# Layer 2's node norms regrouped: late tiles normalised in SBUF with their product and sum on POOL, second norms shared by ACT and DVE

## The chip, the cores and the metric

The kernel runs on one core of one Trainium2 chip. A core has TensorE (PE) for matrix products, VectorE (DVE), ScalarE (ACT) and GpSimd (POOL) for elementwise work, and DMA queues; SP issues plain transfers here and POOL issues the gathers. Each engine works through its own instructions in the order in which they stand, and waits for others by semaphores. SBUF is the on-chip memory of 128 partitions, PSUM the memory into which TensorE writes. The metric is the device time of one execution in microseconds, as the median of several runs; lower is better.

## The reference

Four graph layers work on `x` (8 batches, 2048 nodes, 64 features) with one adjacency matrix. Each layer's output is added to `x`, and the sum is normalised over the features. Only layer 2, the third, is touched:

```python
A = (adj_matrix > 0).astype(x.dtype)
agg = jnp.einsum('ij,bjf->bif', A, x) / jnp.maximum(deg, 1.0)[None, :, None]
out = jax.nn.relu(x @ W_self + b_self + (agg @ W_neigh + b_neigh))
mu = out.mean(axis=-1, keepdims=True)
var = jnp.mean((out - mu) ** 2, axis=-1, keepdims=True)
out = (out - mu) * jax.lax.rsqrt(var + LN_EPS) * ln_gamma + ln_beta   # the first norm
x = _layernorm(x + out, axis=-1)                                      # the second norm
```

## The kernel before

The 2048 nodes are 16 tiles of 128. `X[:, t]` and `S[:, t]` hold tile t in SBUF as 8 batches of 64 features. Before the part in question, each tile of `X` has been turned and multiplied with the weights; `S` holds the self term and `ytab` in memory the neighbours' rows, and `b2` (the norm's beta) has already been added to `X` (line 761).

The neighbour sums of tiles 0 to 8 are made with the adjacency as a matrix (PE, line 899, 144 steps of three matmuls), those of tiles 15 down to 9 with edge lists: `fetch` has POOL issue four gathers of rows of `ytab` for each third of such a tile (helper line 186), and `add_edges` multiplies them with a selection matrix (PE, line 879). The two kinds run interleaved in one loop over the 144 steps.

When a tile's sum in `pa` is complete, `finish` (lines 842 to 854) scales it by the degree and adds the self term (line 844), applies relu (845) and takes statistics with four `bn_stats` (line 780). Tiles that are finished one after the other are put together in groups, whose sizes are in the list `sizes`; a full group starts a `chain`. The order of finishing is 0, 15, 1, 14, 2, 3, 13, 4, 12, 5, 11, 6, 10, 7, 9, 8, and with the sizes 1, 2, 3, 4, 3, 1, 1, 1 the groups are (0), (15, 1), (14, 2, 3), (13, 4, 12, 5), (11, 6, 10), (7), (9), (8).

A `chain` (lines 795 to 823) is a Python generator that emits its instructions piece by piece:

- `newton` (lines 768 to 776): 1/sqrt(variance) for the whole group on DVE, twelve small dependent steps (lines 773, 123, 126 to 128, 775);
- the first norm of each tile, one instruction per batch, from `S` to a PSUM tile `z` (two of these exist, pool `pz`): `scaled` has ACT do it (line 788), or, in a chain that starts when fewer than two sizes are left, DVE every second batch (line 786, argument `shared`): in the trace these are the chains of tiles 7, 9 and 8;
- the product with `g2` (line 809) and the sum with `X` (line 810) on DVE, then statistics of `X` and `newton` again;
- the second norm, in place in `X`, again through `scaled`;
- `show` (lines 825 to 832): POOL copies the tile into one of three buffers `Xo` (line 828) and SP writes it to the table `xtab` in three DMAs (lines 829 and 832).

`advance` moves the chains on: three pieces are emitted for every two steps of the loop, the rest after it, and between pieces come the other matmuls, finishes and gathers. Everything is in a manually scheduled block, so each engine's order is that in which the instructions are emitted: a finish that is emitted after a chain's piece waits behind it on DVE, and gathers emitted after a `show` wait behind its copy on POOL. Beside the steps, PE, ACT and DVE also prepare layer 3: `own_scores` with its DVE reduction (line 701) and `set_shifts` (PE line 705, DVE lines 706 and 710).

After the loop, layer 3 begins with two products (`sides`, PE line 954) whose PSUM results ACT and DVE copy into `U` (lines 963 and 964), and with gathers from `xtab` (the helper's line 186 again, tile `xs`). The gathers need all rows of `xtab`. Instructions of `sides` come into the engines' orders where the planner puts them, not always behind all of layer 2.

Of the kernel before, what the change touches and what calls it, by code (L numbers as in the profile page):

```python
# [21 lines left out]
F32 = mybir.dt.float32  # L22
# [5 lines left out]
AF = mybir.ActivationFunctionType  # L28
ALU = mybir.AluOpType
# [3 lines left out]
P = 128  # L33
# [15 lines left out]
def kernel(ctx: ExitStack, tc: tile.TileContext, ins: dict, out: bass.AP):  # L49
    nc = tc.nc  # L50
    x, adj = ins["x"], ins["adj"]
    B, N, D = x.shape
# [27 lines left out]
    def rows(name, src, pool):  # L80

        n = src.shape[0]
        t = pool.tile([P, n], F32, name=name)
        nc.sync.dma_start(t, src.unsqueeze(0).to_broadcast([P, n]))
        return t

    def over(v, shape):

        for _ in shape[1:-1]:
            v = v.unsqueeze(1)  # L90
        return v.to_broadcast(shape)
# [70 lines left out]
    X = main.tile([P, NT, B, D], F32, name="X")  # L162
# [97 lines left out]
    def node_products(t0, wk, ps):  # L260
# [26 lines left out]
        for q, ph in enumerate(held):  # L287
# [26 lines left out]
                                   op0=ALU.is_equal, op1=ALU.mult)  # L314
# [8 lines left out]
    for it in range(NT):  # L323
# [18 lines left out]
        for k in range(0, SL, 8):  # L342
            nc.vector.max(nbr[:, k:k + 8], topf)
            if k + 8 < SL:
# [19 lines left out]
                                       op0=ALU.is_le, op1=ALU.mult, saturate=False)  # L364
# [27 lines left out]
    held, zs, stats = {}, {}, {}  # L392
# [108 lines left out]
    with ExitStack() as l1:  # L501
# [60 lines left out]
        def finish(it, po):  # L562
            for h in range(2):
                rec = wk.tile([P, HB * D], F32, name="rec")
                nc.vector.reciprocal(rec, po[h][:, 0])  # L565
                nc.vector.tensor_tensor(po[h][:, 1], po[h][:, 1], rec, ALU.mult)
                Xs = X[:, it, h * HB:(h + 1) * HB, :].rearrange("p b d -> p (b d)")
                nc.vector.tensor_tensor(Xs, po[h][:, 1], Xs, ALU.add)
            done.add(it)
            if it ^ 1 in done:  # L570
                layer_norm([X[:, t] for t in (it & ~1, it | 1)], wk)
# [12 lines left out]
        for it in range(FIRST):  # L584
            finish(it, sums[it])
# [13 lines left out]
        def add_edges(n):  # L599
            it, s = quads[n]  # L600
            if s == 0:
                selfs[it] = wk.tile([P, GS, P], F32, name="self_")
                nc.scalar.activation(selfs[it], Sel[:, it], AF.Copy)
                sums[it] = new_sums()
            for h in range(2):
                for g in range(NG):
                    nodes = slice(g * GN, (g + 1) * GN)
                    nc.tensor.matmul(sums[it][h][nodes].rearrange("p a f -> p (a f)"), selfs[it][:, s, nodes],  # L608
                                     rss[n][g][:, h], start=(s == 0), stop=(s == GS - 1))
            if s == GS - 1:  # L610
                finish(it, sums[it])
# [6 lines left out]
        for k, (it, jt) in enumerate(steps):  # L618
            if jt == 0:
                sums[it] = new_sums()  # L620
            add_rows(sums[it], it, jt)
            if jt == NT - 1:
                finish(it, sums[it])
            while n < len(quads) and n * (len(steps) - LATE - EARLY) <= (k - LATE) * len(quads):
                add_edges(n)
                fetch(n + 2)
                n += 1
# [84 lines left out]
    with ExitStack() as l2:  # L712
# [12 lines left out]
        g2 = rows("g2", ins["L2_gnn_ln_gamma"], wp)  # L725
# [7 lines left out]
        S = wp.tile([P, NT, B, D], F32, name="S")  # L733
# [31 lines left out]
        pz = l2.enter_context(tc.tile_pool(name="l2pz", bufs=2, space=PSUM))  # L765
        sums, rss, selfs, shown = {}, {}, {}, []

        def newton(st):

            n = st.shape[1]  # L770
            triples = st.rearrange("p n a (k m) -> p (n a k) m", m=3)
            var, rstd, tmp, nmr = (small.tile([P, 4 * B], F32, name=f"l2_{k}", bufs=4)[:, 0:n * B] for k in "vrtm")
            nc.vector.scalar_tensor_tensor(var, triples[:, :, 2], 1.0 / D, eps.to_broadcast(var.shape), op0=ALU.mult, op1=ALU.add)
            inv_sqrt(rstd, var, tmp)
            nc.vector.scalar_tensor_tensor(nmr, triples[:, :, 1], -1.0, rstd, op0=ALU.mult, op1=ALU.mult)
            return rstd, nmr

        def take_stats(st, k, v):
            for a in range(NP):
                nc.vector.bn_stats(st[:, k, a], v[:, 2 * a:2 * a + 2, :].rearrange("p b d -> p d b"))  # L780

        def scaled(to, v, stats, k, b, shared):
            rstd, nmr = stats
            own = slice(k * B + b, k * B + b + 1)
            if shared and b % 2:
                nc.vector.tensor_scalar(to[:, b], v[:, b], rstd[:, own], nmr[:, own], op0=ALU.mult, op1=ALU.add)
            else:
                nc.scalar.activation(to[:, b], v[:, b], AF.Identity, scale=rstd[:, own], bias=nmr[:, own])  # L788


        sizes = [1, 2, 3, 4, 3, 1, 1, 1]
        together, chains = [], []
        WAIT = 3

        def chain(ts, st):


            shared = len(sizes) < 2
            stats = newton(st)
            for _ in range(WAIT):  # L800
                yield False
            st = small.tile([P, 4, NP, 6], F32, name="l2_sx")[:, 0:len(ts)]
            for k, t in enumerate(ts):
                z = pz.tile([P, B, D], F32, name="z")
                for b in range(B):
                    scaled(z, S[:, t], stats, k, b, shared)
                    if b % 2:
                        yield True
                nc.vector.tensor_tensor(z, z, over(g2, [P, B, D]), ALU.mult)
                nc.vector.tensor_tensor(X[:, t], z, X[:, t], ALU.add)  # L810
                take_stats(st, k, X[:, t])
            stats = newton(st)
            for _ in range(WAIT):
                yield False
            for k, t in enumerate(ts):
                for b in range(B):
                    scaled(X[:, t], X[:, t], stats, k, b, shared)
                    if b % 2:
                        yield True
                    if b == 1 and k:  # L820
                        show(ts[k - 1])
            yield False
            show(ts[-1])

        def show(t):
            Xo = ones_x[len(shown) % len(ones_x)]
            shown.append(t)
            nc.gpsimd.tensor_copy(Xo[:, :, 1:], X[:, t, :, 1:])
            nc.sync.dma_start(xtab[t * P:(t + 1) * P, 0:BD // 2], Xo[:, 0:B // 2].rearrange("p b d -> p (b d)"))
            pair_of = xtab[t * P:(t + 1) * P, BD // 2:].rearrange("n (a k d) -> n a k d", k=2, d=D)  # L830
            for k_ in range(2):
                nc.sync.dma_start(pair_of[:, :, 1 - k_], Xo[:, B // 2 + k_::2])
# [9 lines left out]
        def finish(it):  # L842
            sf = S[:, it].rearrange("p b d -> p (b d)")
            nc.vector.scalar_tensor_tensor(sf, sums.pop(it), r_deg[:, it:it + 1], sf, op0=ALU.mult, op1=ALU.add)
            nc.vector.tensor_scalar(sf, sf, 0.0, None, op0=ALU.max)
            if not together:
                together.append((small.tile([P, 4, NP, 6], F32, name="l2_st")[:, 0:sizes[0]], []))
            st, ts = together[0]
            take_stats(st, len(ts), S[:, it])
            ts.append(it)  # L850
            if len(ts) == sizes[0]:
                sizes.pop(0)
                together.pop()
                chains.append(chain(ts, st))

        by_list = list(range(NT - 1, DENSE - 1, -1))
        quads = [(it, s) for it in by_list for s in range(GS)]
# [78 lines left out]
    with early, ExitStack() as heads:  # L936
# [190 lines left out]
        with tc.manual_schedule(engines=engines):  # L1127
# [22 lines left out]
            t = NT - 1  # L1150
# [10 lines left out]
    with ExitStack() as fifth:  # L1161
# [17 lines left out]
        hss, pes, ws, wxs, zs, stats, sums = ({} for _ in range(7))  # L1179
# [116 lines left out]
        with tc.manual_schedule(engines=engines):  # L1296
# [5 lines left out]
            for u in range(len(units) + 7):  # L1302
# [19 lines left out]
                for plan, t0, t1 in ((after, 0, PAIRED - 2), (sooner, PAIRED - 2, PAIRED)):  # L1322
                    for j, fs in plan.items():
                        k = u - j - 2 * PER + 1
# [3 lines left out]
                for j, fs in alone.items():  # L1328
                    k = u - j - PER + 1
# [35 lines left out]
    with tc.If(bad > 0), ExitStack() as anyway:  # L1365
# [12 lines left out]
        X = main.tile([P, NT, B, D], F32, name="X")  # L1378
# [13 lines left out]
        with tc.tile_pool(name="adjp", bufs=3) as ap_, tc.tile_pool(name="adjps", bufs=4, space=PSUM) as aps:  # L1392
            for it in range(NT):
# [15 lines left out]
                own = ap_.tile([P, P], F32, name="own")  # L1409
# [44 lines left out]
        with ExitStack() as l0:  # L1454
# [71 lines left out]
            for b in range(B):  # L1526
                p, k = divmod(b, 2)
# [8 lines left out]
                for ih in range(2):  # L1536
                    acc = [pa.tile([P, CW], F32, name="acc") for _ in range(2)]
                    for jt in range(NT):
                        w = pp.tile([P, HW], F32, name="w")
                        nc.vector.tensor_scalar(w, F[:, ih * HW:(ih + 1) * HW], Cj[:, jt, b:b + 1], Aj[:, jt, b:b + 1],  # L1540
                                                op0=ALU.mult, op1=ALU.max)
                        nc.vector.scalar_tensor_tensor(w, MT[:, jt, ih * HW:(ih + 1) * HW], 0.0, w,
                                                       op0=ALU.is_equal, op1=ALU.mult)
# [11 lines left out]
                if k == 1:  # L1555
                    for c in range(NCH):
# [4 lines left out]
                        ts = slice(c * TPC, (c + 1) * TPC)  # L1561
                        Xs = X[:, ts, 2 * p:2 * p + 2, :].rearrange("p t b d -> p t (b d)")
                        v = wk.tile([P, TPC, P], F32, name="v", tag="t2")
# [92 lines left out]
        with ExitStack() as l2:  # L1656
# [12 lines left out]
            g2 = rows("g2", ins["L2_gnn_ln_gamma"], wp)  # L1669
            b2 = rows("b2", ins["L2_gnn_ln_beta"], wp)  # L1670

            S = wp.tile([P, NT, B, D], F32, name="S")
# [34 lines left out]
        with ExitStack() as l3:  # L1707
# [44 lines left out]
            bias = wp.tile([D, HN + 1], F32, name="bias")  # L1752
# [149 lines left out]
```

## Time and profile before

| What | us |
|---|---|
| median of five runs | 2067.24 |
| lowest and highest run | 2062.77, 2070.85 |
| the profiled execution: time | 2072.89 |
| the profiled execution: its span | 2071.1 |
| first matmul of layer 2's neighbour sums (line 899) | 823.1 |
| last such matmul begins (line 899) | 976.5 |
| last copy into `Xo` begins (line 828) | 1015.14 |
| first gather of layer 3 (tile `xs`) | 1021.13 |

Over the whole span PE is busy 75%, DVE 68%, POOL 51% and ACT 49%. These shares are means over stages with different limits. Costs of the instructions concerned, as mean or median durations of one:

| Instruction | engine | ns |
|---|---|---|
| line 788, scaling a batch, into `z` (PSUM) | ACT | 408 |
| line 788, scaling a batch, in `X` (SBUF) | ACT | 426 |
| line 786, the same, into `z` | DVE | 347 |
| line 786, the same, in `X` | DVE | 308 |
| lines 809 and 810, product and sum of a tile | DVE | 698, 691 |
| lines 1271 and 1276, product and sum of a tile in layer 3 | POOL | 1277, 1264 |
| line 828, copy of a tile | POOL | 607 |
| line 186, issuing a gather | POOL | 957 |

Instructions in a row overlap a little, so the time from one to the next can be shorter than the duration of one: 32 scalings in `X` on ACT take 10.71 us in a row, 0.335 us each.

### The profile page before, as it was taken

The numbers are of one execution on the slowest core, as the hardware profiler recorded it, in microseconds if no ns is written. First come the engines' busy times: TensorE is split into PE (matmuls) and PEld (weight loads), VectorE is DVE, ScalarE is ACT, GpSimd is POOL, SyncE is SP. The second block draws the span as 40 slices with busy tenths as digits, with TensorE's granted clock in tenths as the row PEclk, the third lists the DMA queues.
The fourth block names the chain that finished last, engine by engine and source line by source line (L and its number), as shares of the span: only waits on it lengthen the run. The fifth ranks groups of instructions, "written<-read, shape, count | busy, mean of one in ns | idle before, by whom it ended". The sixth has DMA issues, their size and how long they took to land.

```text
span 2071.1 us, 35059 instructions
## 1 busy us (share of the span) xinstructions
PE 1557.4 (75%) x13026; PEld 897.7 (43%) x13062; DVE 1414.2 (68%) x3057; ACT 1024.4 (49%) x2504; POOL 1065.1 (51%) x993
## 2 busy tenths in 40 slices
PE   3572344442799987997299999999999689888873
PEld 3562121110333335332188787787787522222210
DVE  6879388886665456557555655656565489889886
ACT  4553144356822234347255545445455246777774
POOL 0000777761655526563245656556555287777760
PEclk9975555665999999999599999999999855555555
DMA  7321666660248942564233323323333165655541
GB/s 198 128 95 61 194 200 206 205 181 24 99 164 294 301 144 89 163 193 122 76 99 109 115 86 109 107 91 109 102 99 111 59 186 154 175 165 166 158 120 22
DMA packets 134243, 283.65 MB, mean 137 GB/s; under 512 B 64145, under 2 KB 66705, under 8 KB 131985
## 3 DMA queue, kind: packets, MB, share of 16 engines
q0 software_dynamic: 64896, 217.10, 34.8%
q1 hardware_dynamic: 52528, 60.03, 8.7%
q10 hardware_dynamic: 16640, 4.20, 0.9%
q8 instruction: 105, 1.72, 0.3%
q14 instruction: 74, 0.60, 0.1%
HBM read 245.35 MB, written 35.91 MB: 136 GB/s over the span
## 4 chain that ended last, share of the span: by engine, by line
PE 38%; DVE 11%; ACT 9%; issue 6%; POOL 6%; DMA 2%; SPq 0%; ACTq 0%; POOLq 0%; DVEq 0%
PE pscore L999 7%; PE pa L556 6%; PE po L1025 6%; PE pt L984 5%; POOL hs L186 3%; PE pm L954 3%; PE pm L1060 3%; PE pa L608 2%; PE pa L899 2%; DVE sc L1204 2%; PE po L1232 1%; ACT z L151 1%; DVE pr L1199 1%; ACT wx L1215 1%; ACT z L788 1%
## 5 line engine op out<-in xcount | busy, mean ns | idle before, releaser
L186 POOL DMA_INDIRECT hs<-htab,src x192 | 183.7, 957 | 269.9 <-PE pe L408 207.5
L1008 DVE SCALAR_TENSOR_TENSOR w<-w,Sel 128x512 f32<-128x512 f32 (+1 forms) x192 | 188.8, 1010 | 173.8 <-ACT w L1002 173.3
L186 POOL DMA_INDIRECT xs<-xtab,src x192 | 221.2, 1152 | 66.9 <-issue 29.7
L556 PE MATMUL pa<-R,ET 128*128 128x512 bf16 x841 | 196.3, 387 | 53.9 <-POOL R L544 34.8
L186 POOL DMA_INDIRECT hs<-ktab,src x192 | 188.6, 982 | 53.8 <-issue 45.8
L999 PE MATMUL pscore<-U,xsT 64*128 64x64 f32 (+1 forms) x3072 | 204.6, 280 | 0.0
L1002 ACT ACTIVATE w<-pscore 128x1024 f32<-128x1024 f32 x128 | 130.9, 1023 | 137.3 <-PE pscore L999 130.2
L999 PEld LDWEIGHTS pscore<-U,xsT 64*128 64x128 f32 x3072 | 183.5, 189 | 21.7 <-issue 15.0
L986 ACT COPY xsT<-pt 128x512 f32<-128x512 f32 x192 | 112.1, 584 | 142.2 <-PE pt L984 140.4
L151 ACT ACTIVATE X<-X,ln_m,ln_r 128x64 f32<-128x64 f32 x256 | 87.2, 427 | 171.4 <-DVE ln_m L143 171.4
L1194 PE MATMUL pe<-hi,selTb 32*128 32x512 bf16 x576 | 135.2, 603 | 35.6 <-DVE pr L1199 34.9
L556 PEld LDWEIGHTS <-ET 128*128 128x128 fp8e4 x864 | 84.1, 99 | 174.5 <-issue 82.8
L1025 PE MATMUL po<-w,xs 128*64 128x64 f32 (+1 forms) x3072 | 143.7, 243 | 16.5 <-DVE o L1030 16.5
L1070 POOL TENSOR_TENSOR h<-h,h2h 128x512 f32<-128x512 f32 x45 | 57.2, 1270 | 165.5 <-DVE h2h L1066 165.3
L1025 PEld LDWEIGHTS po<-w,xs 128*64 128x64 f32 x3072 | 119.5, 137 | 43.9 <-DVE o L1030 18.8
L984 PE MATMUL pt<-ident,xs 128*128 128x128 f32 x768 | 127.8, 290 | 7.7 <-DMA xs<-xtab,src 6.3
L1215 ACT ACTIVATE wx<-hs,w 128x64 f32<-128x64 f32 x512 | 128.7, 341 | 0.1
L1199 DVE TENSOR_TENSOR pr<-pe,hs 128x1024 f32<-128x1024 f32 x96 | 116.7, 1216 | 16.8 <-DMA hs<-ktab,src 10.5
L1204 DVE TENSOR_REDUCE sc<-pr 128x16 f32<-128x1024 f32 x96 | 116.5, 1214 | 4.7 <-ACT w L1206 1.2
L186 POOL DMA_INDIRECT rs<-rtab,src x84 | 79.6, 948 | 71.9 <-PE pa L608 51.8
L565 DVE RECIPROCAL rec<-pa 128x256 f32<-128x256 f32 x32 | 54.1, 1728 | 78.0 <-PE pa L608 48.4
L428 DVE TENSOR_TENSOR hs<-hs,w 128x2048 f32<-128x2048 f32 x48 | 106.7, 2277 | 0.5 <-ACT w L418 0.5
(592 smaller groups left out, 3275.1 us busy)
## 6 DMA issues: line engine op xcount, KB each, us to landing
at<-in_adj SPq DMA_DIRECT2D x16, 1024.0 KB
rtab<-r SPq DMA_DIRECT2D x16, 512.0 KB
ptab<-hp SPq DMA_DIRECT2D x16, 384.0 KB
hi<-ptab SPq DMA_DIRECT2D x16, 384.0 KB
X<-in_x ACTq DMA_DIRECT2D x16, 256.0 KB
htab<-H SPq DMA_DIRECT2D x16, 256.0 KB
ytab<-y SPq DMA_DIRECT2D x16, 256.0 KB
ktab<-hb SPq DMA_DIRECT2D x16, 256.0 KB
```

Of the source, the lines that this page charges most:

```text
L186: nc.gpsimd.indirect_dma_start(out=dst, out_offset=None, in_=table[:, :], in_offset=bass.IndirectOffsetOnAxis(ap=src[:, it, s, g:g + 1], a ...
L556: nc.tensor.matmul(po[h].rearrange("p a f -> p (a f)"), ET[:, jt, it * P:(it + 1) * P], R[:, jt, q, h].rearrange("p a f -> p (a f)"), star ...
L984: nc.tensor.transpose(pt[:, p], xss[k][n][:, p * P:(p + 1) * P], ident)
L986: nc.scalar.copy(xsT, pt)
L999: nc.tensor.matmul(pscore[:, k_, f0:f0 + HN * ni].rearrange("p (h i) -> p h i", i=ni), xsTs[k][t][half, p], Us[it][half, p, :, i0:i0 + ni] ...
L1002: nc.scalar.activation(w.rearrange("p t k a h i -> p k t (a h i)"), pscore.rearrange("p k (t m) -> p k t m", t=n), AF.Exp)
L1008: nc.vector.scalar_tensor_tensor(wt, wt, 3.0e38, edge, op0=ALU.min, op1=ALU.mult)
L1025: nc.tensor.matmul(po[half, p, :, i0:i0 + ni], xss[k][t][:, f0:f0 + D], ws[k][:, t, k_, p], start=(s == 0 and p == 0), stop=(last and p == ...
L1194: nc.tensor.matmul(pe[:, k].rearrange("p b d -> p (b d)"), selTb[nodes, s * P:(s + 1) * P], hi[nodes, q], start=(q == 0), stop=(q == 2))
L1199: nc.vector.tensor_tensor(pr.rearrange("p k b d -> p (k b d)"), pes[u].rearrange("p k b d -> p (k b d)"), hss[u].rearrange("p k b d -> p ( ...
L1204: nc.vector.tensor_reduce(sc, pr, AX.X, ALU.add)
L1215: nc.scalar.activation(wxs[u][:, 0, b], hss[u][:, 0, b], AF.Copy, scale=ws[u][:, 0, b:b + 1])
```

## The change

The sizes become 1, 2, 3, 3, 3, 2, 1, 1, so that the groups are (0), (15, 1), (14, 2, 3), (13, 4, 12), (5, 11, 6), (10, 7), (9), (8). The last three groups, tiles 10, 7, 9 and 8, are `late`.

- First norm, late tiles: in place in `S` in place of the PSUM tile `z`; ACT scales six batches and DVE two (numbers 5 and 7). The product with `g2` and the sum with `X` are POOL's, and a pause in the emission follows before the statistics. The other tiles keep ACT for all eight batches into `z` and DVE for product and sum.
- Second norm: of the other tiles ACT scales batches 0 to 3 and DVE 4 to 7 (before, ACT all eight); of the late tiles ACT six and DVE two (before, ACT all eight of tile 10, and ACT and DVE four each of tiles 7, 9 and 8, as in their first norms).
- A scaled tile is emitted in two pieces of four batches, where it was four pieces of two, in the second norm and in the late first norm.

Lines behind the change move by 14: line 844 becomes 858, 899 becomes 913, 964 becomes 978; line 788 becomes 785, 786 becomes 795, 809 and 810 become 822 and 823.

```diff
-        def scaled(to, v, stats, k, b, shared):
+        def scaled(to, v, stats, k, b):
             rstd, nmr = stats
             own = slice(k * B + b, k * B + b + 1)
-            if shared and b % 2:
-                nc.vector.tensor_scalar(to[:, b], v[:, b], rstd[:, own], nmr[:, own], op0=ALU.mult, op1=ALU.add)
-            else:
-                nc.scalar.activation(to[:, b], v[:, b], AF.Identity, scale=rstd[:, own], bias=nmr[:, own])
-
-
-        sizes = [1, 2, 3, 4, 3, 1, 1, 1]
+            nc.scalar.activation(to[:, b], v[:, b], AF.Identity, scale=rstd[:, own], bias=nmr[:, own])
+
+        def shared(v, stats, k, b, late=False):
+
+            rstd, nmr = stats
+            for b_ in (b, b + 1, b + B // 2, b + B // 2 + 1):
+                own = slice(k * B + b_, k * B + b_ + 1)
+                if b_ < B // 2 or (late and b_ == b + B // 2):
+                    scaled(v, v, stats, k, b_)
+                else:
+                    nc.vector.tensor_scalar(v[:, b_], v[:, b_], rstd[:, own], nmr[:, own], op0=ALU.mult, op1=ALU.add)
+
+
+        sizes = [1, 2, 3, 3, 3, 2, 1, 1]
...
             for k, t in enumerate(ts):
-                z = pz.tile([P, B, D], F32, name="z")
-                for b in range(B):
-                    scaled(z, S[:, t], stats, k, b, shared)
-                    if b % 2:
+                if late:
+                    z = S[:, t]
+                    for b in range(0, B // 2, 2):
+                        shared(z, stats, k, b, late)
                         yield True
-                nc.vector.tensor_tensor(z, z, over(g2, [P, B, D]), ALU.mult)
-                nc.vector.tensor_tensor(X[:, t], z, X[:, t], ALU.add)
+                else:
+                    z = pz.tile([P, B, D], F32, name="z")
+                    for b in range(B):
+                        scaled(z, S[:, t], stats, k, b)
+                        if b % 2:
+                            yield True
+                engine = nc.gpsimd if late else nc.vector
+                engine.tensor_tensor(z, z, over(g2, [P, B, D]), ALU.mult)
+                engine.tensor_tensor(X[:, t], z, X[:, t], ALU.add)
+                if late:
+                    yield False
                 take_stats(st, k, X[:, t])
...
             for k, t in enumerate(ts):
-                for b in range(B):
-                    scaled(X[:, t], X[:, t], stats, k, b, shared)
-                    if b % 2:
-                        yield True
-                    if b == 1 and k:
+                for b in range(0, B // 2, 2):
+                    shared(X[:, t], stats, k, b, late)
+                    yield True
+                    if b == 0 and k:
                         show(ts[k - 1])
...
-                chains.append(chain(ts, st))
+                chains.append(chain(ts, st, len(sizes) < 3))
```

## The prediction

> **What bounds the kernel now.** I read the page first, then the chain of work that ended last over 900 to 1035 us, the engines' busy time in two stretches of layer 2, and the time lines of DVE, POOL and PE there. The change touches only layer 2's node norms, which run from 838 us to the first gather of layer 3 at 1021.13 us. The windows come first (columns: window, length, then busy us of PE, PEld, DVE, ACT, POOL, then granted clock, DMA share, GB/s):
>
> ```profile
> 905.00:976.00 71.00, 63.02 (x267) 22.16 (x270) 46.73 (x166) 41.52 (x113) 37.15 (x42) 0.95 0.54 156
> 976.00:1022.00 46.00, 4.82 (x36) 1.88 (x34) 29.42 (x125) 17.92 (x50) 4.51 (x7) 0.55 0.13 35
> ```
>
> Up to 976 us TensorE is busy 89% of the time. After it, 46 us pass with PE nearly idle and no engine full: this is a tail of dependent norms. The chain of waits (start, length, engine, tile, line) goes through it by ACT and DVE in turn, and ends on the table write:
>
> ```profile
> 949.01 10.71 ACT X L788 x32
> ...
> 976.66 8.06 ACT X L788 x24
> ...
> 1016.15 3.56 DMA xtab<-Xo
> ...
> 1021.13 3.38 DMA xs<-xtab,src
> ```
>
> Layer 3's first gather needs all rows of `xtab`, so whatever moves the last copy into `Xo` moves the rest of the kernel by the same amount. In the time lines the reader should see that the last tile's sum was complete on PE at 976.8, yet its finish on DVE (L844) waited in the queue until 987.77, and 33.4 us lie from there to the gather:
>
> ```profile
> 967.61 9.24 PE L899 MATMUL pa<-Y,ET 128*128 128x512 bf16 x41
> ...
> 987.77 0.74 DVE L844 SCALAR_TENSOR_TENSOR S<-pa,r_deg,S 128x512 f32<-128x512 f32 x1
> ...
> 1015.14 0.61 POOL L828 COPY Xo<-X 128x504 f32<-128x504 f32 x1 [8.28 <-ACT X L788]
> ...
> 1021.13 0.98 POOL L186 DMA_INDIRECT xs<-xtab,src  x1 [5.39 <-issue]
> ```
>
> One more thing decides this case: DVE and POOL get in each other's way. One of Newton's small steps (L128), normally 0.17 us, lasts until the `Xo` copy beside it ends; a DVE addition of two SBUF tiles, normally 0.69 us, starts beside a POOL product and takes 2.38:
>
> ```profile
> 954.54 0.61 POOL L828 COPY Xo<-X 128x504 f32<-128x504 f32 x1 [1.96 <-ACT X L788]
> ...
> 954.60 0.58 DVE L128 SCALAR_TENSOR_TENSOR l_r<-l_t,l_r 128x24 f32<-128x24 f32 x1
> ...
> 2017.85 1.91 POOL L1220 TENSOR_TENSOR wx<-hs,w 128x1024 f32<-128x1024 f32 x1
> ...
> 2017.94 2.38 DVE L1276 TENSOR_TENSOR z<-z,X 128x512 f32<-128x512 f32 x1 [3.06 <-POOL z L1271]
> ```
>
> **What the Trainium skill says.** "SBUF — State Buffer", section "Who interferes with whom": DVE instructions with two SBUF inputs, or in a two-port mode, lock a port pair that POOL shares, and the loser waits for the whole instruction. The trace agrees: 0.58 and 2.38 us above. "GPSIMD Engine Reference", section "4.1 Engine selection": two-input elementwise work is about twice as slow on POOL. Here 1.27 against 0.69 us. "VectorE: DVE Perf Modes", section "Mode 2×_2P — use both read ports for one tensor": an fp32 tensor_scalar in SBUF can take both ports. L845 takes 0.43 us for 512 elements where two-input L810 takes 0.69, which fits; for the 64-element form the trace does not tell. "ScalarE: Activation LUTs", section "Step-by-step: what each stage is for": a PSUM destination is the quicker one. Single instructions agree (408 against 426 ns), but in a row they come every 0.44 us to `z` and every 0.335 us to `X`, so leaving PSUM helps.
>
> **The change part by part.** Prices, all from the rows: ACT to `z` 0.44, in SBUF 0.335; DVE scaling in SBUF 0.225 in a row; L809 0.73, L810 0.73, the four bn_stats of a tile 0.90; Newton's twelve steps 2.3 for one tile, 2.5 for two (between its neighbours), 2.62 for three; finish (L844, L845) 1.2; a POOL product and sum one after the other 2.62 (L1271 at 1733.92 to the end of L1276 at 1736.54); `Xo` 0.61.
>
> Busy time: the twelve early tiles' second norm moves 48 scalings off ACT (-16.1) onto DVE (+10.8). The late tiles move four products and sums off DVE (-5.8) onto POOL (+10.5). None of these sums is on the path as such: ACT and DVE have gaps. What counts is the queues' order, which the built programs show without times. I laid both orders along the prices. For the kernel before this gives the first gather at 1021.25, where the trace has 1021.13; so for the new order the difference is what I use.
>
> - Chain 13, 4, 12 (now three tiles, not four): Newton ends 918.3, 24 scalings to `z` until 929.6, product, sum, statistics and Newton until 934.6. The second norm is quick (ACT 12 x 0.335 = 4.0, was 32 x 0.335 = 10.7), but tile 12's last DVE scalings stand behind the finish of tile 5, so its `Xo` comes at 940.0.
> - Four gathers for PE stand behind that `Xo` on POOL. They now start at 940.6 (before: 928.5), land from 944.9 on, and PE completes tile 6 only at 951.7. PE also waits for L701, which moved behind the same scalings, but no longer than until 940.7: hidden by the gathers. Before, PE waited 5.2 us, at 956.3 to 961.5, for the gathers behind the four-tile chain's copies. In the new order PE ends at 978.6 against 976.8: +1.8, covered, because DVE is later still.
> - Chain 5, 11, 6: Newton 956.6, 24 x 0.44 = 10.6 on ACT, statistics, Newton 972.1; DVE's 12 scalings 2.7; finish of tile 7 at 974.8, Newton of pair 10, 7 at 979.5.
> - First norm of tile 10 in SBUF: ACT 6 x 0.335 = 2.0 beside DVE's two, done 982.0. POOL multiplies and adds until 984.9. Beside it on DVE stand Newton's steps for tile 9, each with two SBUF inputs: with the lock they end at 986.8, without it 984.4. Behind them wait tile 10's statistics and tile 7's two scalings.
> - Tile 7: POOL 988.3 to 991.0, statistics, Newton of the pair until 994.4. Tile 10's second norm 2.0, `Xo` 996.6. Tile 9's product stands behind that copy on POOL (its data were ready at 994.8): 997.2 to 999.8. Statistics and Newton until 1003.1.
> - Only now, behind tile 9's statistics, comes the last finish, tile 8, at 1003.5: 15.7 later than in the trace. The rest is shorter, since no other tile's work is left on DVE: statistics and Newton until 1008.2 (0.2 of it behind `Xo`), ACT 2.0, POOL 2.65, statistics 0.9, one copy of `U` (L964's 0.69, which the new order puts ahead of the last Newton), Newton 2.3, ACT 2.0, `Xo` at 1019.1 to 1019.7, table write and gather 4.9: 1024.6. That is 21.1 after the finish, where 33.4 passed before.
>
> Sum: +15.7 - 12.3 = +3.4 us. Unknown: whether 64-element scalings on DVE also lock. At nothing it stays 3.4; if each one that meets an `Xo` copy waits its 0.6, the same walk gives +5.8. I take the middle, +4.6. The handoff from POOL to DVE is 0.02 us at 572.46 to 572.48, so nothing. Layer 3 starts later by the sum; its own work is not altered, and the copies of `U` that it needs are done before its first rows land. The profiled execution would go from 2072.89 to 2077.5 (span 2071.1 to 2075.7). It lay above the median of the runs; from that I get 2067.24 + 4.6 = 2071.8 us.
>
> **Rivals.** *No lock*: POOL's reads fit between Newton's steps. The 0.58 and 2.38 us above speak against it; for it, only that most steps beside gathers run undisturbed at 0.17 to 0.2. The walk without locks gives 1020.7: -0.5, 2066.7 us. *Slower*: the lock also bites POOL. L1093, the sum with `X` in layer 3, has a median of 1.72 against a minimum of 1.26, since DVE works beside it. If the eight new POOL instructions take 1.72, the walk gives +6.9 without locked scalings and +9.3 with: +8, 2075.2 us. It decides from the point where locked scalings and two stretched instructions meet (5.8 + 2 x 0.46 = 6.7). Against: at the last tile DVE only waits. *Faster*: PE does not wait for the late gathers, because DVE reaches tile 12's last scalings some 9 us before my 940; then PE, chain 5, 11, 6 and the end move forward by up to that, 4.6 - 9 = -4.4, 2062.8 us. Against: 24 scalings to `z` at 0.44, 10.6 us, must lie ahead of them.
>
> **How the numbers follow.** Changes within 0.3% (6.2 us) can't be told from none. The forecast has 0.50, no lock 0.15, slower 0.30, faster 0.05. Of the slower case some 0.25 lies beyond 6.2 us, and of the forecast 0.07, as its upper end is 5.8 and the medians scatter by some 2 us (runs 2062.77 to 2070.85). From the faster case and scatter 0.05 lie below -6.2. That leaves 0.63 for no change. The range reaches from just under no lock to the +9.3 of the slower rival and scatter: 2066 to 2078.
>
> **What would show it.** Right: the last finish on DVE near 1003, after PE has long ended; PE idle about 932 to 945; Newton's steps of 1.2 to 1.4 us beside POOL's products; the first gather at 1024 to 1027. Wrong: Newton's steps at 0.17 beside POOL (no lock), POOL products near 1.7 (slower), or a finish of tile 8 before 998 (faster).

## The result, and the profile after

| | us |
|---|---|
| kernel before, median of 51 runs | 2066.38 |
| changed kernel, median of 30 runs (2065.82 to 2076.92) | 2070.78 |
| ratio, with its 95% interval | 1.002 (1.0013 to 1.0028) |
| forecast: change, time | +4.6, 2071.8 |

The changed kernel is 4.4 us slower (2.7 to 5.8 by the interval), which is inside the bound of no change, 6.2 us.

The two profiled executions can't be compared by their spans: 2071.1 us before, 2063.9 after, the opposite sign. The code up to layer 2 is the same in both, yet the first finish of layer 2 (the scaling of tile 0's complete sum) starts at 837.07 us in the one and at 826.04 in the other. The lines of that finish, before and after:

```profile
837.07 0.75 DVE L844 SCALAR_TENSOR_TENSOR S<-pa,r_deg,S 128x512 f32<-128x512 f32 x1 [0.16 <-PE pa L899]
```

```profile
826.04 0.75 DVE L858 SCALAR_TENSOR_TENSOR S<-pa,r_deg,S 128x512 f32<-128x512 f32 x1 [0.16 <-PE pa L913]
```

Below, times are therefore taken from that first finish. From it to layer 3's first gather it is 184.06 us before and 187.49 after, +3.4; from that gather to the end of the span 1049.97 and 1050.37. So in these two executions the loss lies in layer 2, and layer 3 is as long as it was. To set a time of after beside one of before or of the forecast, 11.03 us are added to it.

The windows of after, moved by 11 us to the same stage, the second with 3 us more at its end so that it reaches layer 3's first gather (columns: window, length, busy us of PE, PEld, DVE, ACT, POOL, then granted clock, DMA share, GB/s):

```profile
894.00:965.00 71.00, 59.38 (x251) 20.75 (x255) 50.29 (x184) 31.09 (x84) 36.64 (x41) 0.93 0.52 151
965.00:1014.00 49.00, 5.95 (x46) 2.47 (x44) 29.18 (x125) 18.35 (x53) 13.64 (x15) 0.59 0.14 36
```

In the first window ACT has 31.09 us to do where it had 41.52: the shared second norm has taken load off it. PE, which was busy 63.02 of 71 us, is down to 59.38, so what ACT was spared did not reach PE. In the second, POOL is busy 13.64 us where it was 4.51; some 10.1 of these are the eight products and sums (1.26 us each). The chain of waits of after ends like this (start, length, engine, tile, line):

```profile
1000.57 1.26 POOL S L822
...
1001.91 1.27 POOL X L823
...
1006.99 2.10 ACT X L785 x6
...
1010.69 1.81 DMA xtab<-Xo
...
1013.53 3.42 DMA xs<-xtab,src
```

POOL now stands in the chain with two pieces. Next, what PE waited for between the first finish and the end of its sums, in the view of waits of after, over 826.04 to 965 us (engine, tile, line, what was waited for: us in total, times, longest):

```profile
PE pm L705 <- DVE pm L701: 7.5, 1, 7.5
PE pa L893 <- DMA rs<-ytab,src: 7.1, 5, 3.0
```

Together 14.6 us. The same view of before, over 837.07 to 976 us, shows 10.1 us for gathers and none for line 701:

```profile
PE pa L879 <- DMA rs<-ytab,src: 10.1, 6, 5.2
```

The time lines of PE, POOL and DVE in after show where the waits come from and what follows:

```profile
929.50 0.59 PE L705 MATMUL pm<-self_sc,mean_row 128*128 128x4 f32 x2 [7.52 <-DVE pm L701]
...
928.98 0.61 POOL L842 COPY Xo<-X 128x504 f32<-128x504 f32 x1 [1.87 <-DVE X L795]
929.74 0.98 POOL L186 DMA_INDIRECT rs<-ytab,src  x1
...
941.54 0.75 DVE L858 SCALAR_TENSOR_TENSOR S<-pa,r_deg,S 128x512 f32<-128x512 f32 x1 [8.79 <-PE pa L913]
...
989.80 0.89 DVE L780 BATCH_NORM_STATS2 l_sx<-X 128x6 f32<-128x128 f32 x4 [4.11 <-POOL X L823]
...
993.65 0.75 DVE L858 SCALAR_TENSOR_TENSOR S<-pa,r_deg,S 128x512 f32<-128x512 f32 x1
...
1009.21 0.60 POOL L842 COPY Xo<-X 128x504 f32<-128x504 f32 x1 [6.03 <-ACT X L785]
1013.53 1.02 POOL L186 DMA_INDIRECT xs<-xtab,src  x1 [3.72 <-issue]
```

The reader should see three things. The gathers for PE start at 929.74, directly behind a copy that waited for a scaling. DVE then idles 8.79 us, since PE completes tile 6 late, and only with its finish at 941.54 can the chain of tiles 5, 11 and 6 begin. And at the end DVE waits 4.11 us for POOL's pair in front of a tile's statistics. The last finish comes 167.61 us after the first (before: 150.70), and from it to the gather it is 19.88 us (before: 33.36).

### The profile page after: what moved, and what is told of

Read it like the earlier page. It is cut to its first block, busy times and chain, and to the rows that moved or that the text cites. A ratio compares the mean times of both kernels' runs of the same rounds, so it can differ in the third digit from the quotient of the medians.

```text
span 2063.9 us, 35066 instructions
## 1 busy us (share of the span) xinstructions
PE 1545.3 (75%) x13026; PEld 888.5 (43%) x13062; DVE 1421.9 (69%) x3089; ACT 1010.5 (49%) x2464; POOL 1075.6 (52%) x1001
## 3 DMA queue, kind: packets, MB, share of 16 engines
q8 instruction: 105, 1.72, 0.3%
## 4 chain that ended last, share of the span: by engine, by line
PE 26%; DVE 8%; ACT 7%; issue 4%; POOL 4%; DMA 2%; ACTq 0%; SPq 0%; POOLq 0%; DVEq 0%
PE pscore L1013 7%; PE po L1039 6%; PE pt L998 5%; PE pm L968 3%; PE pm L1074 3%; POOL hs L186 3%; DVE sc L1218 2%; ACT z L151 2%; ACT wx L1229 2%; DVE pr L1213 1%; PE po L1246 1%; DMA hs<-ktab,src 1%; DVE w L1022 1%; PE pe L1208 1%; POOL wx L1234 1%
## 5 line engine op out<-in xcount | busy, mean ns | idle before, releaser
L186 POOL DMA_INDIRECT xs<-xtab,src x192 | 221.3, 1153 | 65.2 <-issue 27.7
```

What stands on the lines that cost most here:

```text
L186: nc.gpsimd.indirect_dma_start(out=dst, out_offset=None, in_=table[:, :], in_offset=bass.IndirectOffsetOnAxis(ap=src[:, it, s, g:g + 1], a ...
```

## The experiments

The question was where the gain of the regrouping and of the shared norms had gone. Each kernel below computes the full result; each was timed in five rounds beside the kernel before, on the same chip as it, with 4 to 14 runs of each variant. "The walk" is the procedure of the prediction: the instructions of the built program, each engine in its own order, each started when its engine is free and its inputs are there, with the durations of the rows. It was made for each variant ahead of its run. A turn is one time that `advance` moves the chains on: a `yield True` ends the turn, a `yield False` makes the chain pause for it and lets the next chain go on. The last two columns are from the one profiled execution, counted from its first finish.

| kernel | the walk, to before | measured, to before | ratio (95%) | tile 6's finish | first gather of layer 3 |
|---|---|---|---|---|---|
| before | | | | 111.82 | 184.06 |
| changed kernel | +3.4 to +5.8 | +4.4 | 1.0013 to 1.0028 | 115.50 | 187.49 |
| pace | -3.8 | -4.5 | 0.9969 to 0.9988 | 108.94 | 177.84 |
| act2 | +4 | +5.7 | 1.0015 to 1.0034 | 116.50 | 186.23 |
| copies_late | -8 | -7.3 | 0.9949 to 0.9976 | 103.73 | 174.97 |
| dve | -2.4 to 0 | 0.0 | 0.9990 to 1.0007 | 115.25 | 181.75 |
| sizes_only | -5.2 | -6.6 | 0.9944 to 0.9971 | 104.12 | 174.04 |
| old_sizes | -0.5 to +2.5 | +1.4 | 0.9994 to 1.0011 | | 185.66 |
| early_act4_late_dve | -11.5 | -14.6 | 0.9911 to 0.9938 | | 167.74 |
| best1 | -24 | -24.2 | 0.9859 to 0.9889 | | 157.10 |
| best1_pool | -7 | -9.4 | 0.9939 to 0.9965 | | 173.63 |
| best2 | -27.7 | -29.8 | 0.9834 to 0.9866 | | 153.09 |

Where two variants are compared below, it is by their differences to the kernel before in this table. Against the changed kernel the last column agrees with the medians to some 2.5 us, the scatter of a single execution; set against the trace of before it comes out 1 to 3.5 us lower than the medians do, for all but old_sizes, so that execution seems to have been a somewhat long one in this stage. Tile 6's finish is given only where the text uses it; in before DVE had no idle time in front of it (it came straight behind the four-tile chain's second Newton), so PE did not set it there.

**pace: the turns of the loop given back.**

```diff
                     shared(X[:, t], stats, k, b, late)
                     yield True
+                    if not late:
+                        yield True
```

> Edit to the changed kernel: in the second norm of the early tiles each piece of four scalings is followed by a second turn, so that a tile's norm again passes four turns of the edge loop instead of two; nothing else differs, not one instruction is added. Theory A (order of the queues): the changed kernel loses some 9 us because two turns for a tile put the early Xo copies ahead of PE's gathers on POOL and the finishes behind DVE's scalings; then this run is 7.5 to 10 us below the changed kernel, about 3.8 us below the kernel before (2062.5). PE's wait of 7.5 us on L701 before 929.5 should go. Theory B (POOL's slower product and the lock decide alone): no difference to the changed kernel, +4.4 to the kernel before.

Measured: 2061.57 us, 8.9 below the changed kernel. Not one instruction was added or taken away, only the place of some in the queues differs, so B falls. The waits of PE (the view as above, 828.49 to 965 us):

```profile
PE pm L705 <- DVE pm L701: 5.0, 1, 5.0
PE pa L895 <- DMA rs<-ytab,src: 3.9, 3, 3.0
```

The waits went from 14.6 to 8.9 us. The expectation that the one on line 701 would go was wrong: 5.0 of its 7.5 us stayed. Which of the two waits matters was open after this run.

**act2: the load taken off DVE, the turns left.**

```diff
-                    shared(X[:, t], stats, k, b, late)
+                    if late:
+                        shared(X[:, t], stats, k, b, late)
+                    else:
+                        for b_ in range(2 * b, 2 * b + 4):
+                            scaled(X[:, t], X[:, t], stats, k, b_)
```

> Edit to the changed kernel: the second norm of the early tiles is scaled by ACT alone again (48 scalings back from DVE), still in two pieces for a tile. Theory A (order of the queues): the turns are the same as in the changed kernel, so nothing is won or lost by more than 2 us: +4 us to the kernel before. Theory C (the 10.8 us of scalings that DVE took over are what delays its finishes): 5 to 11 us below the changed kernel.

Measured: 2071.69 us, 1.3 above the changed kernel, no difference by the intervals. C falls: taking the 48 scalings off DVE does not shorten the kernel. But the edit also gives them back to ACT, and the run shows two effects that offset each other. PE has no wait of note on line 701 now, so DVE was relieved; instead PE waits longer for gathers, and for them alone (view of waits of act2, 833.88 to 975 us, then its time lines of POOL and PE):

```profile
PE pa L897 <- DMA rs<-ytab,src: 16.6, 7, 6.1
```

```profile
932.39 0.60 POOL L846 COPY Xo<-X 128x504 f32<-128x504 f32 x1 [4.85 <-issue]
935.04 0.61 POOL L846 COPY Xo<-X 128x504 f32<-128x504 f32 x1 [2.05 <-ACT X L785]
937.69 0.61 POOL L846 COPY Xo<-X 128x504 f32<-128x504 f32 x1 [2.04 <-ACT X L785]
938.45 0.98 POOL L186 DMA_INDIRECT rs<-ytab,src  x1 [0.15 <-issue]
...
942.12 1.91 PE L897 MATMUL pa<-rs,self__6276 128*32 128x512 f32 x2 [6.11 <-DMA rs<-ytab,src]
```

POOL does next to nothing from 927.6 to 938.4: it stands at three copies of 0.6 us each, every one of which comes when ACT has done the last of a tile's eight scalings, and the gathers that PE needs stand behind the third. They start 104.6 us after the first finish, where it was 103.7 in the changed kernel: whether ACT alone or ACT and DVE do the scalings, the copies let the gathers go at about the same time.

**copies_late: only the copies moved.** To part the two waits, the early tiles' copies into `Xo` were moved behind eight more turns, and nothing else.

```diff
-                    if b == 0 and k:
+                    if late and b == 0 and k:
                         show(ts[k - 1])
             yield False
+            if not late:
+                for _ in range(8):
+                    yield False
+                for t in ts[:-1]:
+                    show(t)
             show(ts[-1])
```

> Edit to the changed kernel: of the early tiles only the copies into Xo (with their three table writes) move, to eight turns after the chain's last scaling; every scaling, sum and finish keeps its place on ACT and DVE. Theory A1 (the loss comes from Xo copies that stand ahead of PE's gathers on POOL): the walk of the orders gives -8 us to the kernel before, 13 below the changed kernel. Theory A2 (the loss comes from finishes and L701 that stand behind DVE's scalings; POOL's order does not matter): no more than 2 us below the changed kernel, some +3 us to the kernel before.

Measured: 2058.8 us, 7.3 below the kernel before and 11.7 below the changed kernel. A2 falls, for its wait is still there, even longer (view of waits of copies_late, 832.98 to 965 us, then its time line of POOL):

```profile
PE pm L705 <- DVE pm L701: 9.2, 1, 9.2
...
PE pa L898 <- DMA rs<-ytab,src: 0.2, 1, 0.2
```

```profile
922.75 0.95 POOL L186 DMA_INDIRECT rs<-ytab,src  x1 [0.30 <-issue]
...
928.36 0.61 POOL L847 COPY Xo<-X 128x504 f32<-128x504 f32 x1 [1.88 <-DVE X L795]
934.23 0.98 POOL L186 DMA_INDIRECT rs<-ytab,src  x1 [5.26 <-PE pa L898]
```

Now the gathers run ahead of PE until they lack a free buffer (the 5.26 us wait is for PE), and PE's wait for them has shrunk from 7.1 us to 0.2. Tile 6's finish comes 11.8 us earlier after the first finish than in the changed kernel, the whole of the gain. Line 705 also comes earlier (95.9 us after the first finish, 103.5 in the changed kernel), so PE had been held up by such copies before it too. The sum of PE's waits falls by less (14.6 to 9.4 us), because this view leaves out a part. Up to tile 6's finish PE's busy time falls as well, from 99.8 to 93.4 us, and 6.0 of these 6.4 us are in the edge-list matmuls that use the gathered rows (31.5 us in the changed kernel, 25.5 here). Their weight loads (PEld) waited for gathers too, in between (views of waits of the changed kernel, 826.04 to 941.54 us, and of copies_late, 832.98 to 936.71):

```profile
PEld pa L893 <- DMA rs<-ytab,src: 16.8, 15, 2.5
```

```profile
PEld pa L898 <- DMA rs<-ytab,src: 6.1, 10, 1.1
```

That is 10.7 us less, most of the 11.8.

**dve: POOL's part undone.**

```diff
-                engine = nc.gpsimd if late else nc.vector
+                engine = nc.vector
```

> Edit to the changed kernel: product and sum with x of the last four tiles on DVE instead of POOL. Theory A (queue order plus POOL's price): a pair takes 1.4 us on DVE for 2.5 us on POOL, and Newton's steps lose their 2 x 0.95 us of waiting beside POOL; the walk of the orders gives 5.7 us below the changed kernel, level with the kernel before (0 us, or -2.4 if single scalings do not lock). Theory B (POOL's product and the lock decide alone): also 4 to 6 us below the changed kernel; so this run alone does not tell A from B. Theory D (POOL relieves DVE, and giving the work back makes DVE late): no difference to the changed kernel or slower.

Measured: 2065.99 us, level with before and 4.4 below the changed kernel. D falls. Tile 6's finish is where it was (115.25 for 115.50); all of the gain comes after it, in the tail. In dve's time line of DVE a late tile's pair and its statistics follow each other without a gap:

```profile
981.83 0.69 DVE L822 TENSOR_TENSOR S<-S,g 128x512 f32<-128x512 f32 x1
982.55 0.69 DVE L823 TENSOR_TENSOR X<-S,X 128x512 f32<-128x512 f32 x1
983.28 0.88 DVE L780 BATCH_NORM_STATS2 l_sx<-X 128x6 f32<-128x128 f32 x4
```

1.45 us from product to statistics, where the changed kernel needs 2.64 on POOL (1000.57 to 1003.21).

**sizes_only and old_sizes: the regrouping.** The kernel before with the new list of sizes, and the changed kernel with the old one:

```diff
-        sizes = [1, 2, 3, 4, 3, 1, 1, 1]
+        sizes = [1, 2, 3, 3, 3, 2, 1, 1]
```

> Edit to the kernel before: only the list of group sizes is taken from the changed kernel (1,2,3,3,3,2,1,1 for 1,2,3,4,3,1,1,1); all norms as before. Theory A: the walk of the orders gives -5.2 us to the kernel before, so the regrouping is worth something and the rest of the change gives it back. Theory B (sizes are of no account): within 1 us of the kernel before.

> Edit to the changed kernel: the list of group sizes of the kernel before (1,2,3,4,3,1,1,1), so that the last three tiles, each by itself, are the late ones. Theory A, the walk of the orders: +2.5 us to the kernel before (-0.5 if single scalings do not lock), so here the regrouping brings nothing, since the two-turn order eats its gain. If the gain of the sizes (6.6 us alone) simply adds to the rest: +11 us to the kernel before.

Measured: 2059.46 us for sizes_only, 6.6 below the kernel before: one line of the change, alone, is worth more than the whole change loses. The line does a little more than regroup: tile 10 is now in a chain whose norms ACT and DVE share, so that DVE scales 16 batches into `z` and 16 in `X` where it was 12 and 12; no run parts the two. 2067.51 for old_sizes, 1.4 above it. The parts don't add: on top of the rest of the change the new sizes, which there also make tile 10 a late one, cost 3.0 us (4.4 - 1.4) where alone they gain 6.6. The walk is within 1.4 us for sizes_only; for old_sizes the measurement lies between its two ends.

**early_act4_late_dve: what is left when both losses are taken out.** Early tiles as in the kernel before (ACT alone, four turns a tile), late ones in SBUF and shared, on DVE:

```diff
-                engine = nc.gpsimd if late else nc.vector
+                engine = nc.vector
...
-                for b in range(0, B // 2, 2):
-                    shared(X[:, t], stats, k, b, late)
-                    yield True
-                    if b == 0 and k:
-                        show(ts[k - 1])
+                if late:
+                    for b in range(0, B // 2, 2):
+                        shared(X[:, t], stats, k, b, late)
+                        yield True
+                        if b == 0 and k:
+                            show(ts[k - 1])
+                else:
+                    for b in range(B):
+                        scaled(X[:, t], X[:, t], stats, k, b)
+                        if b % 2:
+                            yield True
+                        if b == 1 and k:
+                            show(ts[k - 1])
```

> Edit to the changed kernel: early tiles' second norm as in the kernel before (ACT alone, four turns a tile), and the last four tiles' product and sum on DVE; what stays of the change are the group sizes and the late tiles' norms in SBUF shared between ACT and DVE. Theory A: -11.5 us to the kernel before (the sizes alone gave -6.6, so the SBUF norm at the end is worth some 5). Theory B (a first norm in SBUF is worth nothing at the end): -6.6, as with the sizes alone.

Measured: 2051.53 us, 14.6 below before. B's -6.6 falls; the late tiles' norms in SBUF, shared by ACT and DVE, bring 8.0 us over sizes_only, against some 5 expected. This step also changes the share (six batches to two) and the number of turns of the late tiles, and no run tells how much of the 8.0 us the move from PSUM to SBUF is. Four kernels that each take one step from the last now give the account of the change: sizes -6.6; late norms in SBUF with DVE's product -8.0 (to -14.6); early second norms shared, in two turns, +14.5 (dve, to 0.0); product and sum on POOL +4.4 (the changed kernel). These sizes hold for this sequence of steps, since the parts don't add.

**best1, best1_pool, best2: a version that beats both.** A search with the walk over sizes and waiting turns gave this edit to early_act4_late_dve:

```diff
-        sizes = [1, 2, 3, 3, 3, 2, 1, 1]
+        sizes = [1, 1, 1, 3, 2, 1, 3, 2, 2]
...
-        WAIT = 3
+        WAIT = 4
```

> The kernel of early_act4_late_dve with group sizes 1,1,1,3,2,1,3,2,2 for 1,2,3,3,3,2,1,1 and four turns of waiting after a Newton for three. Theory A, by the walk of the orders: -24 us to the kernel before. If the order of the queues has no more to give (the tail of dependent norms bounds it): -11, as without the new sizes.

Measured: 2041.86 us, 24.2 below before, as forecast to 0.2 us; the second theory falls. With these sizes the last three groups are (5, 11, 6), (10, 7) and (9, 8), so that seven tiles are late where it was four; what the order of the groups, the fourth turn and the three more late tiles bring each, no run separates. best1_pool gives the late products and sums to POOL again (the line of dve, reversed), best2 moves the early copies as copies_late does.

> Edit to best1: product and sum with x of the tiles after the late switch on POOL again, as in the changed kernel. Theory A: here DVE is nowhere late, so each POOL pair is on the path and the statistics of a tile hold up the next tile's scalings on DVE: the walk of the orders gives -7 us to the kernel before, 17 above best1. If POOL's price is only the 1.2 us by which a pair is longer there, for the last chain of two tiles: 2 to 5 above best1.

> Edit to best1: the early tiles' Xo copies moved to eight turns after the chain's last scaling, as in copies_late. Theory A: -27.7 us to the kernel before by the walk of the orders, 3 below best1. If the copies of four-turn tiles no longer stand before gathers that PE lacks: no difference to best1.

Measured: 2055.9 us for best1_pool, 14.8 above best1 (17 forecast, 2 to 5 by the other reading, which falls). In dve's comparison POOL cost 4.4 us. One reason for the larger loss is plain: seven pairs move to POOL here and four there, which makes 2.1 us a pair against 1.1. The time line of DVE shows why a pair costs more:

```profile
968.62 0.88 DVE L780 BATCH_NORM_STATS2 l_sx<-X 128x6 f32<-128x128 f32 x4 [2.78 <-POOL X L823]
969.42 0.52 DVE L795 TENSOR_SCALAR S<-S,l_r,l_m 128x64 f32<-128x64 f32 x2
972.72 0.88 DVE L780 BATCH_NORM_STATS2 l_sx<-X 128x6 f32<-128x128 f32 x4 [2.78 <-POOL X L823]
...
987.18 0.88 DVE L780 BATCH_NORM_STATS2 l_sx<-X 128x6 f32<-128x128 f32 x4 [4.27 <-POOL X L823]
...
991.27 0.88 DVE L780 BATCH_NORM_STATS2 l_sx<-X 128x6 f32<-128x128 f32 x4 [2.78 <-POOL X L823]
```

The next tile's two scalings (969.42) stand on DVE behind the statistics that wait for POOL, so tile after tile goes from DVE to POOL and back: 12.6 us of DVE's waiting in these four lines, 28.8 with the other three late tiles, where the changed kernel has 11.2 for its four. best2 ran in 2035.53 us, 29.8 below the kernel before (ratio 0.985, 0.9834 to 0.9866), the lowest median of all. That is 5.6 below best1, where 3 were forecast; with four runs of each, and intervals that touch, the gain over best1 is likely and its size open (the two traces have 4.0 us). In its view of waits PE waits 0.9 us for gathers in the whole stage:

```profile
PE pa L904 <- DMA rs<-ytab,src: 0.9, 1, 0.9
```

## Why the prediction was right, point by point

The forecast of +4.6 met +4.4, and its steps can be set beside the trace (forecast less 11.03, then measured):

| step as the prediction put it | forecast | trace |
|---|---|---|
| Newton of 13, 4, 12 ends (ACT starts the second norm) | 923.6 | 923.63 |
| gathers behind tile 12's `Xo` start | 929.6 | 929.74 |
| PE completes tile 6 (its finish starts) | 940.7 | 941.54 |
| second Newton of 5, 11, 6 ends | 961.1 | 961.66 |
| finish of tile 7 starts | 963.8 | 965.11 |
| tile 10's product and sum on POOL end | 973.9 | 975.53 |
| Newton of tile 9 ends | 975.8 | 976.96 |
| tile 7 on POOL | 977.3 to 980.0 | 978.33 to 980.93 |
| second Newton of the pair 10, 7 ends | 983.4 | 984.36 |
| `Xo` of tile 10 | 985.6 | 986.61 |
| last finish starts | 992.5 | 993.65 |
| last `Xo` | 1008.1 | 1009.21 |
| first gather of layer 3 | 1013.6 | 1013.53 |

- *The sum.* "+15.7 - 12.3 = +3.4": the trace has +16.9 and -13.5, which is +3.4 too. The order of the queues gave it, not the busy times: that ACT was spared some 16 us of work did not shorten the kernel, and act2, which gives that work back, is level with the changed kernel.
- *The lock on 64-element scalings*, taken at half. They do wait for POOL. In the changed kernel twelve of them beside two `Xo` copies take 3.53 us; in copies_late, where those copies come later, the same twelve take 2.77 (the longest one 0.71 us in the one, 0.31 in the other):

```profile
961.66 3.53 DVE L795 TENSOR_SCALAR X<-X,l_r,l_m 128x64 f32<-128x64 f32 x12
```

```profile
956.90 2.77 DVE L795 TENSOR_SCALAR X<-X,l_r,l_m 128x64 f32<-128x64 f32 x12
```

  That is 0.38 us for each copy met, not the copy's whole 0.6, and it is most of the 1.3 us that the finish of tile 7 is late in the table. It agrees with what the Trainium skill says in "VectorE: DVE Perf Modes", section "Mode 2×_2P — use both read ports for one tensor", that an fp32 tensor_scalar in SBUF can take both read ports, and answers what the trace of before had left open. The first gather is nevertheless where the walk without it put it, because the last table write was quicker in this execution: 4.32 us from the start of the last copy to the gather, against 5.5 in the forecast and 5.99 in the trace of before. A miss of +1.1 us and one of -1.2 cancel there, so it is luck that the gather came within 0.1 us of its forecast, and in part also that +4.6, the middle of two walks, came so close to +4.4.
- *The lock beside POOL's products.* Right, and *no lock* falls. In the time line of after, for tile 9's Newton:

```profile
972.93 1.26 POOL L822 TENSOR_TENSOR S<-S,g 128x512 f32<-128x512 f32 x1 [6.45 <-DVE l_v L773]
...
973.09 1.12 DVE L126 TENSOR_TENSOR l_t<-l_r 128x8 f32<-128x8 f32 x1
974.24 0.17 DVE L127 SCALAR_TENSOR_TENSOR l_t<-l_t,l_v 128x8 f32<-128x8 f32 x1
...
974.26 1.27 POOL L823 TENSOR_TENSOR X<-S,X 128x512 f32<-128x512 f32 x1
...
974.44 1.12 DVE L128 SCALAR_TENSOR_TENSOR l_r<-l_t,l_r 128x8 f32<-128x8 f32 x1
```

  A step of 0.17 us lasts 1.12, once for each instruction of POOL, until that instruction ends: 2 x 0.95 us. (The prediction's sign was a step of 1.2 to 1.4 us.) The step at 974.24 slips through the gap between the two. This is what the Trainium skill's "SBUF — State Buffer", section "Who interferes with whom", says of the loser's wait.
- *Slower* supposed that the lock stretches POOL's eight instructions to 1.72 us. All eight took 1.26 to 1.27, so it falls; DVE was the side that waited.
- *Leaving PSUM helps ACT.* 24 scalings to `z` took 10.33 us in a row (0.43 each), 12 in SBUF 4.09 (0.34), as priced. That this made the kernel faster no run shows by itself.
- *Where the reasoning was incomplete.* The prediction had the gathers behind tile 12's `Xo`, but called PE's delay "+1.8, covered, because DVE is later still". DVE was later because of PE: it idled 8.79 us before tile 6's finish. copies_late shows that nothing covered it: taking the copies from in front of the gathers moved the whole end by 11.7 us. The *Faster* rival had the size of this lever (9 us) but looked for it in DVE's reaching tile 12's scalings; the lever is the copies' place on POOL.

## What to carry to other kernels

On an in-order engine an instruction that waits for others is as long as its wait, to everything behind it (three copies of 0.6 us held POOL for 10.8 us in act2): put it behind the work that a busy engine needs (here gathers for TensorE), even if that makes it later. When a piece of code that is emitted between other work is made coarser, its instructions and their copies move in several queues at once, and this can cost more than the balanced load brings; list the queues before and after. And a product that is twice as slow on another engine can cost more than the difference when other work stands in the queue behind its result: seven pairs, each 1.2 us longer on POOL, cost 14.8 us in best1_pool, four cost 4.4 in the changed kernel.

## What the runs showed of the hardware

TensorE ran slower after an idle stretch, and the granted clock shows it. The first nine matmuls of the dense sums after line 705 took 4.00 us where PE had waited 7.52 us in front of it, and 2.10 in sizes_only, where it had waited 1.19. The time lines of the changed kernel and of sizes_only:

```profile
929.94 4.00 PE L913 MATMUL pa<-Y,ET 128*128 128x512 bf16 x9
```

```profile
933.23 2.10 PE L899 MATMUL pa<-Y,ET 128*128 128x512 bf16 x9
```

The windows, first of the changed kernel (early in the wait, late in it, and the nine matmuls), then of sizes_only (the nine matmuls), with the granted clock in the last column but two (the counts take in neighbours at the edges):

```profile
922.00:925.00 3.00, 0.00 (x0) 0.00 (x0) 2.72 (x15) 1.37 (x5) 0.00 (x0) 1.00 0.01 3
926.00:929.50 3.50, 0.00 (x1) 0.01 (x1) 3.43 (x13) 1.71 (x6) 1.12 (x2) 0.50 0.54 147
929.94:933.94 4.00, 4.00 (x11) 1.23 (x12) 2.62 (x15) 0.00 (x0) 3.09 (x4) 0.50 0.67 175
```

```profile
933.23:935.33 2.10, 2.10 (x15) 0.85 (x18) 1.97 (x10) 2.10 (x7) 0.32 (x1) 1.00 0.33 98
```

The granted clock fell from 1.00 to 0.50 during the wait and was still at 0.50 under the nine matmuls, so here the wait cost 1.9 us beyond its own length. The same nine took 4.00 us in pace and in dve (after waits of 4.99 and 7.69 us), 3.66 in copies_late (after 9.19), and 2.10 in before and in act2, where there was no such wait. Between a wait of 1.19 us, after which they ran at full clock, and one of 4.99, after which they did not, no run here lies.
